# Two cross-attention layers on one core: first-layer probabilities computed a second time with keys on the partitions, in place of transposing them

## The chip, the cores and the metric

The kernel runs on one core of one Trainium2 chip. The metric is the device time in microseconds. The engines are TensorE (PE, its weight loads PEld), VectorE (DVE), ScalarE (ACT), GpSimd (POOL) and SyncE (SP); here SP issues nearly all loads and POOL nearly all stores.

## The reference

Two layers of cross-attention over 8 batches, each with 100 queries of width 640 (20 heads of 32), a context of 722 tokens of width 1024, of which the first 77 are "text" and the other 645 are "ip" tokens. Each layer has two softmaxes per head, one over the 77 text tokens and one over the 645 ip tokens, and adds their results. The first layer, cut to what matters:

```python
text = encoder_hidden_states[:, :TEXT_LEN, :]           # 77 tokens
ip = encoder_hidden_states[:, TEXT_LEN:, :]             # 645 tokens
q = split_heads(hidden_states @ Wq.T)
k, v = split_heads(text @ Wk.T), split_heads(text @ Wv.T)
out_text = merge_heads(softmax(q @ k.T * scale) @ v)
k_ip, v_ip = split_heads(ip @ Wk_ip.T), split_heads(ip @ Wv_ip.T)
out_ip = merge_heads(softmax(q @ k_ip.T * scale) @ v_ip)
out = (out_text + out_ip) @ Wo.T + bo + residual
```

The second layer has the same shape. Its ip scores get an added term from a further text attention, and its ip probabilities are multiplied by a mask per query. All data is float32.

## The kernel before

**Visits.** The attention work is cut into 80 visits (u, c): u from 0 to 15 is a batch in a layer (0 to 7 the first layer, 8 to 15 the second), c from 0 to 4 a chunk of 128 channels, which is four heads. A visit handles 100 queries, four heads, 722 keys.

**What a visit computes.** `scores(u, c, part)` multiplies q and k with the queries on the partitions: part 0 covers keys 0 to 511, part 1 keys 512 to 721 (ip 512 to 644 and the text). Each head lies on 32 partitions of q and k, so four products use four row groups of the array. The results go to two PSUM tiles `sc0` and `sc1` (two heads each, one buffer each), which both parts use in turn. DVE takes the maxima (L1001 of part 0 and 1, L1022 of the text), ACT the exponentials with their sums (L1015), each part under its own maximum. `factors()` (L1037 to L1041) turns the sums and the two maxima into one factor for each query, head and part, and ACT (L1047, `scaled`) and DVE (L1055, L1051, `scaled_rest`) multiply the probabilities p by them. In the following visit, `transposes` (L1096) turns p in six blocks of keys: blocks 0 to 4 of 128 ip keys, block 5 of the last 5 ip keys and the 77 text keys. Each block is four transposes (one per head) and one copy from PSUM to `pt` (L1101 on ACT for blocks 2 and 4, L1103 on DVE for the others). Then `values` (L1119) multiplies `pt` with v, 24 products into one PSUM tile, and DVE copies the result to `hs` (L1123). So a visit holds its own scores and the transposes and values of the visit before.

**Beside it.** Between these pieces PE computes the k and v of the pair of batches that comes next (`psk` L667, `psv` L637), with Strassen-like sums: seven steps a to e in two PSUM buffers, each of them ended by an addition on DVE or a copy on ACT (L202 to L233, the eviction; a step of the first layer's v also evicts a text part, L623 to L627). Some visits also hold pieces of the output product (`pso` L904) and of the next layer's q (`psq` L923).

**Order.** PE, DVE and ACT run in the order in which the program issues their work. The order of a visit is fixed: part 0 of the scores, tasks, transposes 0 and 1, tasks, transposes 2 and 3, part 1, tasks, transposes 4 and 5, tasks, values. `spread` decides how many product tasks fall into each gap: it takes a fixed own time per visit (5.3) and levels the sums. Work on ACT and DVE that follows the scores is put on a list `later` and issued piece by piece, one piece in front of each product task (`emit(1)` in `next_task`), or all of it at fixed places. The queues of SP and POOL are ordered by a scheduler that goes by modelled times. Loads of k (`load_k`, two buffers), v (`load_v`, two buffers) and blocks of the context (`load_x`, three places) are all in SP's queue. The probabilities p have two buffers, `pt` has one.

Of the kernel before, what the change touches and what calls it, by code (L numbers as in the profile page):

```python
# [14 lines left out]
P = 128  # L15
B = 8
# [30 lines left out]
def two_layer_xattn(  # L47
# [35 lines left out]
    k_d = [dram.tile([P, NC_, NI], F32, tag=f"k_{u}", name=f"k_d{u}") for u in range(NU)]  # L83
    v_d = [dram.tile([NB * P, C], F32, tag=f"v_{u}", name=f"v_d{u}") for u in range(NU)]
    g_d = [dram.tile([2, NI, NT], F32, tag=f"g_{g}", name=f"g_d{g}") for g in range(B // 2)]

    ident = const.tile([P, P], F32, tag="ident", name="ident")
    make_identity(nc, ident)
# [876 lines left out]
        nc.sync.dma_start(out[LAST[i] % B], resg[g][:, i])  # L965


    pr, stats, sct = {}, {}, {}

    later = []  # L970

# [8 lines left out]
    def scores(u, c, part):  # L980
        k0, k1 = ((0, KA), (KA, NK))[part]
        if part == 0:
            pr[u, c] = ppool.tile([S, 4, NK], F32, tag="p", name=f"p_{u}_{c}")

            stats[u, c] = stat.tile([S, 14, 4], F32, tag="st", name=f"st_{u}_{c}")
        else:
            free_scores()

        scs = [ps_sc.tile([P, 2, 512], F32, tag=f"sc{h}", name=f"sc_{u}_{c}_{part}_{h}") for h in range(2)]
        for i in range(4):  # L990
            rows = slice(32 * i, 32 * i + 32)
            nc.tensor.matmul(  # L992
                scs[i // 2][:S, i % 2, : k1 - k0], lhsT=qs_[u][rows, c, :], rhs=ks[u, c][rows, k0:k1], start=True, stop=True
            )
        p, st, l = pr[u, c], stats[u, c], u // B
        n = min(k1, NI) - k0
        lo, f, rz, mul = st[:, 6, :], st[:, 7:9, :], st[:, 9:11, :], st[:, 11:13, :]

        def maxima(h):
            if l == 0:  # L1000
                nc.vector.tensor_reduce(  # L1001
                    st[:, part, 2 * h : 2 * h + 2], scs[h][:S, :, :n], AX.X, ALU.max, negate=True
                )
                return
            for i in (2 * h, 2 * h + 1):

                nc.vector.tensor_tensor_reduce(  # L1007
                    out=p[:, i, k0 : k0 + n], in0=scs[h][:S, i % 2, :n], in1=sems[u][:, k0 : k0 + n], scale=-1.0,
                    scalar=3.0e38, op0=ALU.add, op1=ALU.min, accum_out=st[:, part, i : i + 1],
                )  # L1010

        def exponentials(h):
            for i in (2 * h, 2 * h + 1):
                dst = p[:, i, k0 : k0 + n]
                nc.scalar.activation(  # L1015
                    dst, dst if l else scs[h][:S, i % 2, :n], AF.Exp, bias=st[:, part, i : i + 1],
                    scale=-1.0 if l else 1.0, accum_out=st[:, 3 + part, i : i + 1],
                )

        def text_maxima(h):  # L1020
            heads = slice(2 * h, 2 * h + 2)
            nc.vector.tensor_reduce(st[:, 2, heads], scs[h][:S, :, n:KB], AX.X, ALU.max, negate=True)  # L1022
            nc.vector.tensor_tensor(
                p[:, heads, NI:], scs[h][:S, :, n:KB], st[:, 2, heads].unsqueeze(2).to_broadcast([S, 2, NT]), ALU.add
            )

        def differences():

            nc.vector.tensor_tensor(lo, st[:, 0, :], st[:, 1, :], ALU.min)
            nc.vector.tensor_tensor(f, lo.unsqueeze(1).to_broadcast([S, 2, 4]), st[:, 0:2, :], ALU.subtract)  # L1030

        def text_exponentials():
            nc.scalar.activation(f, f, AF.Exp)
            nc.scalar.activation(p[:, :, NI:], p[:, :, NI:], AF.Exp)

        def factors():
            nc.vector.tensor_reduce(st[:, 5, :], p[:, :, NI:], AX.X, ALU.add)  # L1037
            nc.vector.tensor_tensor(st[:, 3:5, :], st[:, 3:5, :], f, ALU.mult)
            nc.vector.tensor_tensor(st[:, 4, :], st[:, 3, :], st[:, 4, :], ALU.add)
            nc.vector.reciprocal(rz, st[:, 4:6, :])  # L1040
            nc.vector.scalar_tensor_tensor(  # L1041
                mul, f, mask_sb[:, l : l + 1], rz[:, 0:1, :].to_broadcast([S, 2, 4]), ALU.mult, ALU.mult
            )

        def scaled(heads):
            for i in heads:
                nc.scalar.activation(p[:, i, :KA], p[:, i, :KA], AF.Copy, scale=mul[:, 0, i : i + 1])  # L1047

        def scaled_rest(text):
            if text:  # L1050
                nc.vector.tensor_tensor(  # L1051
                    p[:, :, NI:], p[:, :, NI:], rz[:, 1, :].unsqueeze(2).to_broadcast([S, 4, NT]), ALU.mult
                )
            else:
                nc.vector.tensor_tensor(  # L1055
                    p[:, :, KA:NI], p[:, :, KA:NI], mul[:, 1, :].unsqueeze(2).to_broadcast([S, 4, NI - KA]),
                    ALU.mult,
                )

        for h in range(2):  # L1060
            maxima(h)
        if part == 0:
            later.append((True, lambda: exponentials(0)))
            later.append((True, lambda: exponentials(1)))
        else:
            for h in range(2):
                text_maxima(h)
            differences()
            later.append((True, lambda: (exponentials(0), exponentials(1), text_exponentials())))
            if (u, c) == ORDER[-1]:  # L1070

                later.append((False, lambda: (
                    factors(), scaled((0, 1)),
                    nc.vector.tensor_tensor(
                        p[:, 2:, :KA], p[:, 2:, :KA], mul[:, 0, 2:].unsqueeze(2).to_broadcast([S, 2, KA]), ALU.mult
                    ),
                    scaled_rest(False), scaled_rest(True),
                )))
                return
            later.append((False, lambda: (factors(), scaled_rest(False))))  # L1080
            later.append((False, lambda: (scaled((0, 1)), scaled_rest(True))))
            later.append((False, lambda: scaled((2, 3))))

    pts = {}

    def transposes(u, c, j, at_end=False):
        if j == 0:
# [17 lines left out]
    def values(u, c):  # L1105
        g, at = group_of[u]
        if g not in hsg:

            hsg[g] = one.tile([P, 2, NC_, S], F32, tag="hs" if g < len(PAIRS) - 1 else "qst", name=f"hs_{g}")
        pt = pts[u, c]  # L1110
        ps = ps_pt.tile([P, 512], F32, tag="pt", name=f"pv_{u}_{c}")
        for j in range(6):
            for i in range(4):
                if j < 5:
                    lhs = vs[u, c][:, j, i * D : (i + 1) * D]
                else:
                    lhs = vts[u][:, (4 * c + i) * D : (4 * c + i + 1) * D]
                rows = P if j < 5 else NTAIL
                nc.tensor.matmul(  # L1119
                    ps[32 * i : 32 * i + 32, :S], lhsT=lhs, rhs=pt[:rows, j, i * S : (i + 1) * S],  # L1120
                    start=(j == 0), stop=(j == 5),
                )
        nc.vector.tensor_copy(hsg[g][:, at, c, :], ps[:, :S])  # L1123


    AHEAD = 1.2
# [63 lines left out]
    def spread(a, b, tasks):  # L1190

        parts = [(max(a, n), min(b, n + 1)) for n in range(math.floor(a), math.ceil(b))]
        own = [(hi - lo) * (5.3 + small_time(math.floor(lo))) for lo, hi in parts]
        total = sum(t for t, _ in tasks)
        level = (total + sum(own)) / (b - a)
        while True:
            room = [max(0.0, level * (hi - lo) - o) for (lo, hi), o in zip(parts, own)]
            if sum(room) <= total * 1.001:
                break
            level *= 0.999  # L1200
        placed, done, i, before = [], 0.0, 0, 0.0
        scale = sum(room) / total
        for t, f in tasks:
            at = done * scale
            while i < len(parts) - 1 and at >= before + room[i]:
                before += room[i]
                i += 1
            lo, hi = parts[i]
            placed.append((t, lo + (hi - lo) * min(1.0, (at - before) / max(room[i], 1e-9)), f))
            done += t  # L1210
        return placed
# [74 lines left out]
    with tc.manual_schedule(engines=PINNED):  # L1286
# [45 lines left out]
        for n, (u, c) in enumerate(ORDER):  # L1332
# [3 lines left out]
            if n == len(ORDER) - 1:  # L1336
                load_v(*last)
                load_v(u, c)
            between(n, 0.0, 0.4, at[0])
            if last:  # L1340
                transposes(*last, 0)
                transposes(*last, 1)
            between(n, 0.4, 0.6, at[1])
            if last:
                transposes(*last, 2)
                transposes(*last, 3)
            scores(u, c, 1)
# [7 lines left out]
            if n + 1 < len(ORDER):  # L1355
                load_k(*ORDER[n + 1])
            if last:
                transposes(*last, 4)
                transposes(*last, 5)
            if few:  # L1360
                between(n, 0.6, 0.8, at[2])
# [58 lines left out]
```

## Time and profile before

| what | value |
|---|---|
| median of 3 runs | 2047.32 us (2045.9 to 2048.35) |
| the profiled execution | 2048.29 us, its span 2046.5 us |
| granted TensorE clock | 0.998 |
| PE, DVE, ACT, POOL busy | 2027.1, 1130.6, 783.0, 274.1 us |
| first-layer visits (0,0) to (7,4) | 405.26 to 1338.82 us of the span |
| PE busy in them | 932.44 of 933.56 us |
| p's transposes (L1096), all visits | 1920, 211.5 us on PE |
| scores (L992), all visits | 1280 instructions, 138.6 us on PE |
| scaling of p on ACT (L1047) | 318 of 713 ns |
| copies to pt: DVE L1103, ACT L1101 | 319 of 568 ns, 161 of 491 ns |

The busy time of a group is the union of its instructions' times; mean ns is that of one instruction. Products that run side by side on several row groups have a mean much longer than their share of the busy time. A float32 product is two instructions in the trace, a transpose is one. "Idle before" is the engine's idle time ahead of a group and what ended it.

### The profile page before, as it was taken

To read this page: it belongs to the slowest core of one execution; us is meant where nothing else is said; L and a number is where in the kernel's file an instruction comes from. 1 tells how busy PE (TensorE), PEld (TensorE's weight loads), DVE (VectorE), ACT (ScalarE), POOL (GpSimd) and SP (SyncE) were. 2 spreads that over 40 slices of the span, in tenths; PEclk is the share of its full clock that TensorE was granted. 3 is DMA by queue.
4 is the path that set the end of the run, shared out by engine and by line. 5 is a ranking of instruction groups with operands and counts; after the bars stand their busy time and mean duration, and the time that the engine had idled before them with its cause. 6 is when DMAs were issued, how large, how long until landed. Compare 5 with 4: busy or idle time off the path is not lost.

```text
span 2046.5 us, 38708 instructions
## 1 busy us (share of the span) xinstructions
PE 2027.1 (99%) x15162; PEld 1573.3 (77%) x15162; DVE 1130.6 (55%) x3047; ACT 783.0 (38%) x2245; POOL 274.1 (13%) x433
## 2 busy tenths in 40 slices
PE   9999999999999999999999999999999999999998
PEld 9676768776876867778678777777777778888877
DVE  2223322246555455554657665656665667778787
ACT  1001000033433343333434344444543545556675
POOL 0001212111111101111111001001011111111110
PEclk9999999999999999999999999999999999999999
DMA  9544323323432533225245353326332535555461
GB/s 343 151 135 147 102 75 93 99 74 90 117 99 74 155 95 110 86 89 166 79 136 162 106 155 113 95 91 180 107 106 89 152 105 152 161 141 139 124 184 52
DMA packets 296484, 252.20 MB, mean 123 GB/s; under 512 B 46638, under 2 KB 265442, under 8 KB 296302
## 3 DMA queue, kind: packets, MB, share of 16 engines
q1 hardware_dynamic: 274254, 181.19, 31.9%
q0 software_dynamic: 21776, 68.44, 9.2%
q8 instruction: 119, 1.95, 0.4%
q14 instruction: 63, 0.52, 0.1%
q10 hardware_dynamic: 272, 0.10, 0.0%
HBM read 180.74 MB, written 68.93 MB: 122 GB/s over the span
## 4 chain that ended last, share of the span: by engine, by line
PE 95%; DVE 4%; ACT 1%; issue 0%; DMA 0%; SPq 0%; DVEq 0%
PE psv_a L637 9%; PE psv_d L637 8%; PE pspt L1096 8%; PE psk_a L667 8%; PE psk_d L667 7%; PE sc L992 6%; PE pv L1119 4%; PE psv_e L637 4%; PE psk_b L667 4%; PE psk_c L667 4%; PE psv_b L637 4%; PE psv_c L637 4%; PE psk_e L667 4%; PE pso L904 3%; PE psq L923 2%; PE psq L305 2%
## 5 line engine op out<-in xcount | busy, mean ns | idle before, releaser
L1015 ACT ACTIVATE p<-sc,st 100x512 f32<-100x512 f32 (+1 forms) x320 | 165.5, 529 | 202.3 <-DVE st L1001 120.5
L1047 ACT ACTIVATE p<-p,st 100x512 f32<-100x512 f32 x318 | 206.7, 713 | 50.9 <-DVE st L1041 50.6
L1096 PEld LDWEIGHTS pspt<-ident,p 100*128 100x128 f32 (+1 forms) x1920 | 189.0, 138 | 43.3 <-issue 5.5
L1103 DVE COPY pt<-pspt 128x400 f32<-128x400 f32 (+1 forms) x319 | 175.3, 568 | 83.8 <-PE pspt L1096 75.3
L1096 PE MATMUL pspt<-ident,p 100*128 100x100 f32 (+1 forms) x1920 | 211.5, 252 | 6.8 <-DVE pt L1103 2.1
L1015 ACT ACTIVATE p<-p,st 100x512 f32<-100x512 f32 (+1 forms) x320 | 176.6, 554 | 78.2 <-DVE st L1007 78.1
L637 PE MATMUL psv_a<-wv,x 128*128 128x397 f32 (+1 forms) x560 | 185.8, 474 | 0.6 <-DVE ko L228 0.3
L1101 ACT COPY pt<-pspt 128x400 f32<-128x400 f32 x161 | 79.1, 491 | 268.4 <-PE pspt L1096 268.0
L637 PE MATMUL psv_d<-wv,s 128*128 128x320 f32 (+1 forms) x560 | 174.5, 454 | 0.0
L691 POOL DMA_DIRECT2D k_d<-ko x140 | 100.0, 718 | 453.5 <-DVE ko L228 399.8
L637 PEld LDWEIGHTS psv_a<-wv,x 128*128 128x128 f32 x560 | 103.2, 190 | 68.5 <-issue 13.3
L1007 DVE CUSTOM_DVE_ANT_0 p<-sc,sem 100x512 f32<-100x512 f32 (+1 forms) x320 | 138.7, 490 | 21.9 <-PE sc L992 21.0
L637 PEld LDWEIGHTS psv_d<-wv,s 128*128 128x128 f32 x560 | 103.8, 190 | 51.8 <-issue 2.5
L1001 DVE TENSOR_REDUCE st<-sc 100x2 f32<-100x1024 f32 (+1 forms) x160 | 125.3, 824 | 28.8 <-PE sc L992 28.7
L992 PE MATMUL sc<-k,q 32*100 32x210 f32 (+1 forms) x1280 | 138.6, 502 | 0.0
L667 PE MATMUL psk_d<-s,wk 128*128 128x256 f32 (+1 forms) x672 | 136.7, 349 | 0.1
L667 PE MATMUL psk_a<-x,wk 128*128 128x256 f32 (+1 forms) x672 | 135.2, 346 | 0.0
L667 PEld LDWEIGHTS psk_d<-s,wk 128*128 128x128 f32 x672 | 108.6, 189 | 20.6 <-issue 6.7
L667 PEld LDWEIGHTS psk_a<-x,wk 128*128 128x128 f32 x672 | 109.6, 189 | 17.6 <-issue 4.5
L652 POOL DMA_DIRECT2D v_d<-vo x70 | 38.8, 554 | 624.6 <-DVE gst L627 318.6
L637 PE MATMUL psv_e<-wvt,x 128*128 128x397 f32 (+1 forms) x280 | 92.9, 474 | 0.0
L1119 PEld LDWEIGHTS pv<-pt,v 128*32 128x32 f32 x3200 | 67.7, 110 | 26.0 <-issue 16.3
(218 smaller groups left out, 3306.0 us busy)
## 6 DMA issues: line engine op xcount, KB each, us to landing
x<-ip_t SPq DMA_DIRECT2D x80, 512.0 KB
k<-k_d SPq DMA_DIRECT2D x80, 322.5 KB
v<-v_d SPq DMA_DIRECT2D x80, 320.0 KB
v_d<-vo POOLq DMA_DIRECT2D x70, 320.0 KB, 2.4
k_d<-ko POOLq DMA_DIRECT2D x112, 128.0 KB, 4.1
o<-wo SPq DMA_DIRECT2D x35, 320.0 KB
x<-ip_t SPq DMA_DIRECT2D x20, 532.0 KB
q<-wq SPq DMA_DIRECT2D x20, 320.0 KB
```

The costliest lines, as they stand in the source:

```text
L637: nc.tensor.matmul(ps[:, :m], lhsT=tokens(k)[:, :P], rhs=w[:, k, :], start=(k == 0 and not go_on), stop=(k == HK - 1), skip_group_check=True,)
L667: nc.tensor.matmul(ps[:, i * m : (i + 1) * m], lhsT=w[:, k, :], rhs=tokens(k), start=(i == 0 and k == 0 and not go_on), stop=(k == HK - 1) ...
L691: nc.gpsimd.dma_start(dst[:, :, r], src)
L992: nc.tensor.matmul(scs[i // 2][:S, i % 2, : k1 - k0], lhsT=qs_[u][rows, c, :], rhs=ks[u, c][rows, k0:k1], start=True, stop=True)
L1001: nc.vector.tensor_reduce(st[:, part, 2 * h : 2 * h + 2], scs[h][:S, :, :n], AX.X, ALU.max, negate=True)
L1007: nc.vector.tensor_tensor_reduce(out=p[:, i, k0 : k0 + n], in0=scs[h][:S, i % 2, :n], in1=sems[u][:, k0 : k0 + n], scale=-1.0, scalar=3.0e ...
L1015: nc.scalar.activation(dst, dst if l else scs[h][:S, i % 2, :n], AF.Exp, bias=st[:, part, i : i + 1], scale=-1.0 if l else 1.0, accum_out= ...
L1047: nc.scalar.activation(p[:, i, :KA], p[:, i, :KA], AF.Copy, scale=mul[:, 0, i : i + 1])
L1096: nc.tensor.transpose(ps[:rows, i * S : (i + 1) * S], pr[u, c][:, i, j * P : j * P + rows], ident[:S, :S])
L1101: nc.scalar.copy(dst, src)
L1103: nc.vector.tensor_copy(dst, src)
L1119: nc.tensor.matmul(ps[32 * i : 32 * i + 32, :S], lhsT=lhs, rhs=pt[:rows, j, i * S : (i + 1) * S], start=(j == 0), stop=(j == 5),)
```

## The change

In the first layer (u below 8), p is no longer scaled and its blocks 0 to 4 are no longer transposed. Instead:

- `finished` runs after part 1: it computes the factors, scales only block 5's part of p (5 ip keys and the text), and stores 8 numbers per query to DRAM: the negated maximum over both parts and the inverse of the sum, each for four heads (`st_d`, alternating between two tensors).
- `load_stats` loads them back in the next visit, from SP's queue: the maxima spread over all 128 partitions, the inverse of each head over that head's 32 partitions. They land in the space of p (which now has 128 partitions) that is free by then.
- `key_scores` computes the scores again in the place of transposes 0 and 1, with keys on the partitions: 5 blocks by 4 heads, k as the weights and q moving. The results lie in the same two PSUM tiles that the two parts of the scores use. For each pair of heads, DVE adds the maxima (128x1000) and ACT takes the exponential, into `pt`.
- `values` sums blocks 0 to 4 and block 5 apart; DVE multiplies the first by the inverse and adds the second.
- `spread` takes 4.6 as the own time of a first-layer visit.

The first scores, their maxima, exponentials and sums stay; so do the transposes of block 5, and the whole second layer.

```diff
+    st_d = [dram.tile([2, 4, S], F32, tag=f"st_{i}", name=f"st_d{i}") for i in range(2)]
...
-            pr[u, c] = ppool.tile([S, 4, NK], F32, tag="p", name=f"p_{u}_{c}")
+            wholes[u, c] = ppool.tile([P, 4, NK], F32, tag="p", name=f"p_{u}_{c}")
+            pr[u, c] = wholes[u, c][:S]
...
+        def finished():
+
+            factors()
+            nc.vector.tensor_tensor(
+                p[:, :, P * NB : NI], p[:, :, P * NB : NI],
+                mul[:, 1, :].unsqueeze(2).to_broadcast([S, 4, NL]), ALU.mult,
+            )
+            scaled_rest(True)
+            nc.sync.dma_start(st_d[(NC_ * u + c) % 2].rearrange("r i q -> q r i"), st[:, 8:10, :])
...
             later.append((True, lambda: (exponentials(0), exponentials(1), text_exponentials())))
+            if l == 0:
+                later.append((False, finished))
+                return
...
+    def load_stats(u, c):
+
+        whole, src = wholes[u, c], st_d[(NC_ * u + c) % 2]
+        nc.sync.dma_start(whole[:, :, :S], src[0].unsqueeze(0).to_broadcast([P, 4, S]))
+        for i in range(4):
+            nc.sync.dma_start(
+                whole[32 * i : 32 * i + 32, :, S : S + S // 4],
+                src[1, i].rearrange("(a q) -> a q", a=4).unsqueeze(0).to_broadcast([32, 4, S // 4]),
+            )
+
+    def key_scores(u, c):
+
+        emit(len(later))
+        pts[u, c] = one.tile([P, 6, 4 * S], F32, tag="pt", name=f"pt_{u}_{c}")
+        scs = [ps_sc.tile([P, 2, 512], F32, tag=f"sc{h}", name=f"sck_{u}_{c}_{h}") for h in range(2)]
+        for j in range(NB):
+            for i in range(4):
+                rows = slice(32 * i, 32 * i + 32)
+                nc.tensor.matmul(
+                    scs[i // 2][:, i % 2, j * S : (j + 1) * S], lhsT=ks[u, c][rows, j * P : (j + 1) * P],
+                    rhs=qs_[u][rows, c, :], start=True, stop=True,
+                )
+
+        def exponentials(h):
+            dst = pts[u, c][:, :NB, 2 * h * S : 2 * (h + 1) * S]
+            nc.vector.tensor_tensor(
+                dst.rearrange("p j (i q) -> p i j q", q=S),
+                scs[h][:, :, : NB * S].rearrange("p i (j q) -> p i j q", q=S),
+                wholes[u, c][:, 2 * h : 2 * h + 2, :S].unsqueeze(2).to_broadcast([P, 2, NB, S]), ALU.add,
+            )
+            nc.scalar.activation(dst, dst, AF.Exp)
+
+        for h in range(2):
+            later.append((True, lambda h=h: exponentials(h)))
...
+                q0 = S if apart and j == 5 else 0
                 nc.tensor.matmul(
-                    ps[32 * i : 32 * i + 32, :S], lhsT=lhs, rhs=pt[:rows, j, i * S : (i + 1) * S],
-                    start=(j == 0), stop=(j == 5),
+                    ps[32 * i : 32 * i + 32, q0 : q0 + S], lhsT=lhs, rhs=pt[:rows, j, i * S : (i + 1) * S],
+                    start=(j == 0 or q0 > 0), stop=(j == 5 or apart and j == 4),
                 )
-        nc.vector.tensor_copy(hsg[g][:, at, c, :], ps[:, :S])
+        hs = hsg[g][:, at, c, :]
+        if apart:
+            nc.vector.tensor_tensor(
+                hs.rearrange("p (a q) -> p a q", a=4), ps[:, :S].rearrange("p (a q) -> p a q", a=4),
+                wholes[u, c][:, :, S : S + S // 4], ALU.mult,
+            )
+            nc.vector.tensor_tensor(hs, hs, ps[:, S : 2 * S], ALU.add)
+        else:
+            nc.vector.tensor_copy(hs, ps[:, :S])
...
-        own = [(hi - lo) * (5.3 + small_time(math.floor(lo))) for lo, hi in parts]
+        own = [(hi - lo) * ((4.6 if lo < NC_ * B else 5.3) + small_time(math.floor(lo))) for lo, hi in parts]
...
+            first = last and last[0] < B
+            if first:
+                load_stats(*last)
             between(n, 0.0, 0.4, at[0])
-            if last:
+            if first:
+                key_scores(*last)
+            elif last:
                 transposes(*last, 0)
                 transposes(*last, 1)
             between(n, 0.4, 0.6, at[1])
-            if last:
+            if last and not first:
                 transposes(*last, 2)
                 transposes(*last, 3)
             scores(u, c, 1)
...
             if last:
-                transposes(*last, 4)
+                if not first:
+                    transposes(*last, 4)
                 transposes(*last, 5)
```

More of the change, by code (lines that the diff above doesn't have):

```diff
@@ L965, in last_out_add @@
         nc.sync.dma_start(out[LAST[i] % B], resg[g][:, i])
-    pr, stats, sct = {}, {}, {}
+    pr, stats, wholes = {}, {}, {}
     later = []
@@ L996, in scores @@
         n = min(k1, NI) - k0
-        lo, f, rz, mul = st[:, 6, :], st[:, 7:9, :], st[:, 9:11, :], st[:, 11:13, :]
+        lo, f, rz, mul = st[:, 8, :], st[:, 6:8, :], st[:, 9:11, :], st[:, 11:13, :]
         def maxima(h):
@@ L1111, in values @@
         ps = ps_pt.tile([P, 512], F32, tag="pt", name=f"pv_{u}_{c}")
+        apart = u < B
         for j in range(6):
```

## The prediction

> **What bounds the kernel now.** I read the page first: busy shares, then the chain that ended last.
>
> ```profile
> span 2046.5 us, 38708 instructions
> ...
> PE 2027.1 (99%) x15162; PEld 1573.3 (77%) x15162; DVE 1130.6 (55%) x3047; ACT 783.0 (38%) x2245; POOL 274.1 (13%) x433
> ...
> PE 95%; DVE 4%; ACT 1%; issue 0%; DMA 0%; SPq 0%; DVEq 0%
> ```
>
> TensorE is busy 99% of the span and 95% of the chain. A share is a mean over stages, so I asked for the busy times of the stretch that the change touches (the 40 first-layer visits, 405.26 to 1338.82 us) and for PE's waits inside it.
>
> ```profile
> core 0: us, PE busy (x) PEld busy (x) DVE busy (x) ACT busy (x) POOL busy (x), PEclk, DMA share, GB/s
> ...
> 405.26:1338.82 933.56, 932.44 (x6746) 708.21 (x6745) 527.86 (x1239) 370.59 (x1087) 126.03 (x202) 1.00 0.38 110
> ```
>
> ```profile
> PE psv_a L637 <- DVE ko L228: 0.3, 1, 0.3
> PE pspt L1096 <- DVE res L909: 0.2, 1, 0.2
> ```
>
> PE idles 1.1 us in 933.6. So only PE time counts here: a microsecond of PE work taken away is a microsecond won, a new PE wait is a microsecond lost, and DVE, ACT and DMA count only through waits that they put on PE. What separates PE from such waits is read in the timeline, here the shortest first-layer visit, (2,3).
>
> ```profile
> 722.12 1.12 PE L992 MATMUL sc<-k,q 32*100 32x512 f32 x8
> ...
> 723.17 2.42 PE L637 MATMUL psv_c<-wvt,x 128*128 128x320 f32 x8
> ...
> 725.43 0.85 PE L1096 MATMUL pspt<-ident,p 100*128 100x100 f32 x8
> ...
> 726.11 2.86 PE L637 MATMUL psv_d<-wv,s 128*128 128x397 f32 x8
> ...
> 727.11 0.21 ACT L1015 ACTIVATION_READ_ACCUMULATOR p<-sc,st 100x1 f32 x1
> ...
> 728.81 0.85 PE L1096 MATMUL pspt<-ident,p 100*128 100x100 f32 x8
> ...
> 729.01 0.49 DVE L222 TENSOR_TENSOR vo<-psv_d,vo 128x320 f32<-128x320 f32 x1 [1.33 <-PE psv_d L637]
> ...
> 729.42 0.23 DVE L625 COPY gst<-psv_d 128x77 f32<-128x77 f32 x1
> ...
> 729.60 0.61 PE L992 MATMUL sc<-k,q 32*100 32x210 f32 x8
> ```
>
> The second part of the scores starts at 729.60 into the same two PSUM tiles whose exponentials ended at 727.3: 2.3 us to spare in the tightest visit. Eight transposes take 0.68 us from start to next start (725.43 to 726.11), 85 ns each.
>
> [...]the 32x100 load of sc takes 160 ns, the 100-column load of psm 168. [...]eight sc products of 502 ns mean come one set in 1.05 us (722.12 to 723.17). [...]DVE's rows stand in program order. [...]
>
> **The change, part by part**, for 40 visits, in the instruction order of the changed program.
>
> *PE, removed.* Blocks 0 to 4, four heads: 20 transposes a visit, 800 x 85 ns = 68 us. Block 5's four stay.
>
> *PE, added.* 20 second scores a visit, 40 instructions (each f32 product is two), weights 32x128, 100 columns moving, four row groups at once: 10 rounds. A round's length isn't shown. Moving 100 columns takes 85 ns (as the transposes)[...]. Nearest row: L956, 128-column weights with 100 moving:
>
> ```profile
> 2016.36 2.40 PE L956 MATMUL pso_last<-hs,wol 128*128 128x100 f32 x20
> 2018.68 1.07 PE L1119 MATMUL pv<-pt,v 128*32 128x100 f32 x40
> ```
>
> 2.32 us for 20, 116 ns. I take 10 x 116 + 0.35 for entering and leaving the tiled group (sc's 210-column set takes 0.54 us for 2 x 175 ns, and its successor's first product 0.1 more) = 1.5 us, 60 us in all. Low end 10 x 85 + 0.3 = 1.15 (46 us); high end 1.75 (70 us), if loads do not overlap. PE work: -8 us (-22 to +2).
>
> *DVE and ACT, off the path as sums.* Per visit DVE loses three copies (L1103, 570 ns) and L1055 (712), gains two additions of 128x1000, one more operation at PV's result (260) and a small scaling. An addition: 421 ns at 256 columns and 491 at 320 (L207, L222) give 1.09 ns a column, so 1.23 us (L1001 reads 1024 in 1.22). Net +0.5 us of a 23 us visit. ACT loses four scalings (714) and two copies (491), gains two exponentials of about 1.1 us: -1.6. Both are idle over 40% of the stretch; cover holds. What matters is where they stand.
>
> *New wait A: the second part of the scores.* Second scores use the two score tiles between the two parts, so part 1 must wait for both additions. They are emitted one per product task: head pair 0's before the first task, pair 1's before the second. **With only one task in between, pair 1's addition stands in DVE's FIFO behind that task's eviction, which waits for the task's end.** PE then waits 0.20 (end to eviction, 728.81 to 729.01) + 0.41 + 0.23 where the text part is evicted too + 1.23 + about 0.1 = 1.9 to 2.2 us. In the changed order this is so in 13 visits: (0,3), (1,2), (1,3), (2,3), (3,3), (4,3), (5,3), (5,4), (6,3), (6,4), (7,1), (7,2), (7,4). 13 x 2.0 = 26 us. About 15 others have two pieces of which the second lasts 1.7 us against the 2.0 needed: 4 us; (7,3), with two block sums of 0.7 us in between, 1.2. Sum 31 us (24 to 38).
>
> *New wait B: the second scores themselves.* They need the tiles when the first part's exponentials are done, and stand where the first transposes stood (which needed only ps_pt). In (2,3), (4,3), (6,3) one task of 2.13 us comes before: PE would be there at 725.4, exponentials end at 727.3, 1.9 us. In (6,4) that task's copy also stands in ACT's queue: 2.8. Sum 8 us (6 to 10). Others have two to four tasks, 4.3 us and more, against 4.2.
>
> *New wait C: the maxima by way of DRAM.* The first addition waits for a store and a load on SP's queue, and all of DVE's queue, the task evictions first, waits behind it. Chain from the end of part 1: factors done after 4.8 us (visit (7,0): 1243.84 to L1041's end 1248.65), two scalings 0.6, the store of 800 four-byte elements, the load. By the page's stores (1.9 to 6.6 us to landing)[...] I estimate 6 (3 to 9) and 3.5 (2.5 to 6): landed after 15 (11 to 20). Wanted: summing PE's own durations from part 1 to the end of the next visit's second scores gives 16 to 23 us in 36 visits, 13.5 to 14.7 in (0,1), (2,4), (4,4), 10.6 plus wait B in (6,4), each with 1.2 us more before PE notices. So 3 us in all; at 20 us most visits lose about 1: 40.
>
> *SP's queue.* Six DMAs a visit, 240. K's load now waits for the second scores (two buffers): issued near the middle of the visit, at least 9 us ahead of its use; in (2,3) before, it was issued at 730.30 and used at 737.05 without a wait. V is read at the end of the next visit. Block loads that end up behind the store have over 20 us (issued 697.00 and 706.29, first read 732.37). I cost these at nothing. What is queued behind the store's wait is then at worst late by the rest of one visit.
>
> *Spacing (4.6 for 5.3).* It moves one task across a border in five of the visits from (8,0) on: nothing.
>
> Sum against the profiled execution's 2048.3 us: -8 + 31 + 8 + 3 = +34, 2082; its time is 1 us above the median of 2047.3, so 2081.
>
> **Rivals.** (1) *PE's saving wins* (faster). The round is 85 ns: 22 us are saved at the second scores. It decides if waits A to C stay below 22 us, for A under about 1 us a single-task visit. For it: the removed work is certain, and four-row tiling does work in sc. Against: A's order in DVE's queue is fixed, and 1.23 us of it is the addition alone. About 2040. (2) *The round trip is late*: first additions wait for DMA in most visits and every eviction with them; at 20 us 2120, at 25 us five more for 40 visits, 2300. For it: 800 four-byte elements, none seen before; against: the slack above. (3) *Waits and savings cancel*: 22 saved, 24 lost: 2049.
>
> **How the numbers follow.** Main case 0.72 (2060 to 2105, likeliest 2081); rival 2 0.16; rival 1 0.08; rival 3 0.04. Range 2057 to 2120: it takes the main case with its bounds and half of rival 2. About 0.2% (4 us) is what a measurement of this kernel can tell from no change; slower 0.88, same 0.04, faster 0.08.
>
> **What would show it.** In the changed profile: second scores of 1.5 us a visit; PE idle in the first layer up from 1 to over 35 us, ended by DVE pt (the additions) ahead of part 1 of the scores in the thirteen visits and by ACT p ahead of the second scores in four; visit (2,3) near 18 us instead of 14.9; hardly any DVE idle ended by a DMA. I am wrong if PE's idle there stays under 20 us, if a round takes 85 ns, or if the additions wait for DMA in most visits.

## The result, and the profile after

The changed kernel takes 2099.12 us (median of 4 runs, 2097.04 to 2107.21) against 2047.17 us for the kernel before (4 runs): a ratio of 1.0261 (95% interval 1.0233 to 1.0289). It is slower, as forecast, and 18 us slower than the 2081 us that the sum gave. The profiled execution took 2097.04 us, its span 2095.3 us, with a granted clock of 0.990 where it was 0.998.

The page of the changed kernel: the span, the engines' busy times, and the chain that ended last by engine.

```profile
span 2095.3 us, 40740 instructions
...
PE 2047.6 (98%) x15962; PEld 1561.0 (75%) x15962; DVE 1147.6 (55%) x3047; ACT 727.9 (35%) x2085; POOL 273.9 (13%) x433
...
PE 90%; DVE 5%; DMA 3%; ACT 1%; issue 1%; DVEq 0%; SPq 0%; ACTq 0%
```

PE's busy time grew by 20.5 us although work was taken from it; DVE and, newly, DMA stand in the chain. The same stretch as before, the 40 first-layer visits, in the windows view of the changed kernel:

```profile
core 0: us, PE busy (x) PEld busy (x) DVE busy (x) ACT busy (x) POOL busy (x), PEclk, DMA share, GB/s
404.83:1389.53 984.70, 956.12 (x7527) 700.69 (x7526) 545.02 (x1238) 314.17 (x927) 126.03 (x202) 0.98 0.52 114
```

The stretch is 51.1 us longer (984.7 for 933.6); all else in the span is 2.3 us shorter. PE is idle for 28.6 us in it instead of 1.1. That is only 27.5 of the 51.1 us. The other 23.7 us are PE busy longer, and the column to look at is PEclk: 0.98 where it was 1.00. PE's waits in the stretch (the waits view: engine, line waited for, total, times, longest):

```profile
PE sc L994 <- DVE pt L1126: 21.3, 23, 1.4
PE sck L1119 <- ACT p L1017: 6.8, 8, 1.2
```

These are the waits A (and C) and B of the prediction, at their places. PE's rows of visit (2,3), from the timeline of the changed kernel (start, length, line, tile, count, and in brackets the idle time before it with its releaser):

```profile
729.76 1.12 PE L994 MATMUL sc<-k,q 32*100 32x512 f32 x8
730.81 2.42 PE L638 MATMUL psv_c<-wvt,x 128*128 128x320 f32 x8
733.83 0.47 PE L1119 MATMUL sck<-q,k 32*128 32x100 f32 x4 [0.59 <-ACT p L1017]
735.16 1.36 PE L1119 MATMUL sck<-q,k 32*128 32x100 f32 x36 [0.87 <-ACT p L1017]
736.45 2.94 PE L638 MATMUL psv_d<-wv,s 128*128 128x397 f32 x8
739.32 0.60 PE L994 MATMUL sc<-k,q 32*100 32x210 f32 x4
741.32 0.60 PE L994 MATMUL sc<-k,q 32*100 32x210 f32 x4 [1.39 <-DVE pt L1126]
741.85 4.63 PE L638 MATMUL psv_e<-wvt,x 128*128 128x397 f32 x8
```

Read the last three lines together. Part 1 of the scores ran in two sets of four products, 0.60 us each, where all eight side by side took 0.61: the split costs 0.6 us that no wait shows. Between the sets PE waits 1.39 us for pair 1's addition. And then the eight products of `psv_e`, of the same form as `psv_d` above (2.94 us), take 4.63 us. Nothing is late in that row. The windows view over those microseconds shows why:

```profile
741.85:742.35 0.50, 0.50 (x3) 0.38 (x2) 0.39 (x2) 0.39 (x1) 0.00 (x0) 0.66 0.06 20
742.35:745.35 3.00, 3.00 (x6) 1.50 (x5) 2.65 (x9) 1.97 (x10) 0.00 (x0) 0.50 0.01 3
745.35:746.35 1.00, 1.00 (x5) 0.50 (x4) 0.00 (x0) 0.00 (x0) 0.00 (x0) 0.96 0.00 0
```

PEclk (third column from the end) is 0.50: the clock was halved for 3.41 us, from 742.01 to 745.43 in the trace's record of the clock. There are 12 such stretches of 3.41 us in the changed kernel's first layer and none in that of the kernel before; each takes 1.7 us, as `psv_e` did here (4.63 us for 2.94), 20.5 us in all. The cost of the split sets is read from the groups of part 1's products, before and after (busy time, mean ns of one):

```profile
L992 PE MATMUL sc<-k,q 32*100 32x210 f32 x640 | 49.2, 377 | 0.0
L994 PE MATMUL sc<-k,q 32*100 32x210 f32 x640 | 60.7, 376 | 21.5 <-DVE pt L1126 21.3
```

That is 11.5 us. The second scores, split in four visits, are busy 55.4 us in this first layer, and 53.7 in the run below where none of them is split (e8): 1.7 us more. So the 51.1 us are: half clock 20.5, idle 27.5, split sets about 13, and PE's own work, about 10 us less (below): together 51.

### The profile page after: what moved, and what is told of

The parts are those of the page before. It is cut to its first block, busy times and chain, and to the rows that moved or that the text cites. A ratio compares the mean times of both kernels' runs of the same rounds, so it can differ in the third digit from the quotient of the medians.

```text
span 2095.3 us, 40740 instructions
## 1 busy us (share of the span) xinstructions
PE 2047.6 (98%) x15962; PEld 1561.0 (75%) x15962; DVE 1147.6 (55%) x3047; ACT 727.9 (35%) x2085; POOL 273.9 (13%) x433
## 4 chain that ended last, share of the span: by engine, by line
PE 90%; DVE 5%; DMA 3%; ACT 1%; issue 1%; DVEq 0%; SPq 0%; ACTq 0%
PE psv_d L638 8%; PE psk_d L668 8%; PE psv_a L638 7%; PE psk_a L668 7%; PE sc L994 6%; PE psv_e L638 4%; PE pspt L1146 4%; PE pv L1172 4%; PE psk_c L668 4%; PE psk_b L668 4%; PE psk_e L668 3%; PE psv_b L638 3%; PE psv_c L638 3%; PE pso L905 3%; PE sck L1119 2%; DMA st_d<-st 2%
## 5 line engine op out<-in xcount | busy, mean ns | idle before, releaser
L638 PE MATMUL psv_d<-wv,s 128*128 128x320 f32 (+1 forms) x560 | 180.0, 465 | 0.0
L994 PE MATMUL sc<-k,q 32*100 32x210 f32 (+1 forms) x1280 | 150.1, 502 | 21.5 <-DVE pt L1126 21.3
L1131 ACT ACTIVATE pt<-pt 128x1000 f32<-128x1000 f32 x80 | 83.0, 1037 | 251.8 <-DVE pt L1126 251.7
L1009 DVE CUSTOM_DVE_ANT_0 p<-sc,sem 100x512 f32<-100x512 f32 (+1 forms) x320 | 138.7, 490 | 21.1 <-PE sc L994 20.1
L668 PE MATMUL psk_d<-s,wk 128*128 128x256 f32 (+1 forms) x672 | 142.5, 360 | 0.0
L1153 DVE COPY pt<-pspt 128x400 f32<-128x400 f32 (+1 forms) x199 | 110.1, 567 | 45.6 <-PE pspt L1146 43.0
L1146 PE MATMUL pspt<-ident,p 100*128 100x100 f32 (+1 forms) x1120 | 127.4, 251 | 7.0 <-DVE pt L1153 2.1
L1146 PEld LDWEIGHTS pspt<-ident,p 100*128 100x128 f32 (+1 forms) x1120 | 109.2, 135 | 30.7 <-issue 4.2
L1126 DVE TENSOR_TENSOR pt<-sck,p 128x1000 f32<-128x1000 f32 x80 | 95.2, 1194 | 64.1 <-DMA p<-st_d 37.3
L1049 ACT ACTIVATE p<-p,st 100x512 f32<-100x512 f32 x158 | 102.8, 713 | 30.1 <-DVE st L1043 29.8
L638 PE MATMUL psv_e<-wvt,x 128*128 128x397 f32 (+1 forms) x280 | 98.3, 495 | 0.0
```

The source lines that it names most:

```text
L638: nc.tensor.matmul(ps[:, :m], lhsT=tokens(k)[:, :P], rhs=w[:, k, :], start=(k == 0 and not go_on), stop=(k == HK - 1), skip_group_check=True,)
L668: nc.tensor.matmul(ps[:, i * m : (i + 1) * m], lhsT=w[:, k, :], rhs=tokens(k), start=(i == 0 and k == 0 and not go_on), stop=(k == HK - 1) ...
L994: nc.tensor.matmul(scs[i // 2][:S, i % 2, : k1 - k0], lhsT=qs_[u][rows, c, :], rhs=ks[u, c][rows, k0:k1], start=True, stop=True)
L1009: nc.vector.tensor_tensor_reduce(out=p[:, i, k0 : k0 + n], in0=scs[h][:S, i % 2, :n], in1=sems[u][:, k0 : k0 + n], scale=-1.0, scalar=3.0e ...
L1126: nc.vector.tensor_tensor(dst.rearrange("p j (i q) -> p i j q", q=S), scs[h][:, :, : NB * S].rearrange("p i (j q) -> p i j q", q=S), whole ...
L1146: nc.tensor.transpose(ps[:rows, i * S : (i + 1) * S], pr[u, c][:, i, j * P : j * P + rows], ident[:S, :S])
```

## The experiments

Three theories. **Order**: the waits stem from where the additions stand (A), where the second scores stand (B), and little from the round trip (C). **Round trip**: the maxima come late from DRAM, for DVE's idle time says so. **Work**: the second scores are dearer than the transposes, for PE's busy time rose. A fourth came from the reading above, **clock**: a wait also costs the half-clock stretch that may follow it. The line for the round trip, from DVE's waits in the changed kernel's first layer:

```profile
DVE pt L1126 <- DMA p<-st_d: 37.3, 12, 6.4
```

### Idle work on TensorE (e3)

`LONE` lists the thirteen single-task visits of the prediction.

```diff
+    def fill(visit, n):
+        ps = ps_pt.tile([P, 512], F32, tag="pt", name=f"fill_{visit[0]}_{visit[1]}_{n}")
+        for _ in range(n):
+            nc.tensor.matmul(ps[:, :S], lhsT=ident, rhs=ident[:, :S], start=True, stop=True)
...
+            if i == 2 and part == 1 and (u, c) in LONE:
+                fill((u, c), 4)
...
+                if (i, j) == (2, 0) and now in ((2, 3), (4, 3), (6, 3), (6, 4)):
+                    fill(now, 2)
```

> Idle work is added to TensorE and nothing is taken away: in the 13 single-task visits four products of the identity with itself (128x128 by 100 columns, some 0.23 us each) between the first and second head pair of part 1 of the scores, and two of them between the head pairs of the second scores in (2,3), (4,3), (6,3), (6,4); nobody reads their result. Clock theory[...]: 9 to 11 of the 12 windows go, the waits stay as long as they are: 2099 - 17 = 2082 (2077 to 2088). Waiting theory (the waits alone are the loss, the half-clock records follow from something else): no gain; 60 products of 0.23 us lie in the waits or add up to 5 us: 2098 to 2105, and the half-clock windows stay.

Measured: 2081.14 us, ratio to before 1.0162 (1.0146 to 1.0177): 18 us faster than the changed kernel, with 60 products more. The same visit in its timeline, and its first layer in the windows view:

```profile
735.26 0.60 PE L1003 MATMUL sc<-k,q 32*100 32x210 f32 x4
735.79 1.14 PE L976 MATMUL fill<-ident 128*128 128x100 f32 x8
737.26 0.60 PE L1003 MATMUL sc<-k,q 32*100 32x210 f32 x4 [0.33 <-DVE pt L1137]
737.79 2.94 PE L638 MATMUL psv_e<-wvt,x 128*128 128x397 f32 x8
```

```profile
405.21:1371.93 966.72, 953.66 (x7646) 702.78 (x7646) 544.86 (x1238) 314.07 (x927) 126.36 (x202) 1.00 0.50 116
```

The second set of scores starts 2.00 us after the first, as in the changed kernel (739.32 to 741.32): the wait is as long as it was, only filled. But `psv_e` is back at 2.94 us, and one half-clock stretch is left of 12. So the clock's share is shown, 18 us of the total, by a run that takes away neither a wait nor any work of the changed kernel.

### Half of that work (e10)

> As the run with idle work on TensorE, with half of it: two products instead of four in the 13 single-task visits, one instead of two in the four visits of the second scores. The gaps ahead of part 1 keep some 0.9 us instead of 0.4. If a window halves the next one's clock only from an idle time of 1.1 us on (none of some 100 windows with 0.2 to 1.1 us of idle did so in the traces so far), this is as fast as the full filler but for late-maxima windows: 2083 (2080 to 2088). If every microsecond of idle counts in proportion, half of the 18 us gained are lost: 2090.

Measured: 2081.31 us, 1.0164 (1.0149 to 1.0180), the same as with the full filler. PE's idle time is more than in that run, as these waits of the half filler's first layer show (8.0 and 2.7 us in those two lines there), and it costs nothing:

```profile
PE sc L1003 <- DVE pt L1137: 13.2, 18, 2.9
PE sck L1130 <- ACT p L1026: 4.0, 8, 0.8
```

This is what the first of the two readings expected (2083), where loss in proportion would have given 2090. So the clock was not lost in proportion to the idle time here; the last section counts how much idle time stood ahead of the half-clock stretches.

### Additions together (e1)

```diff
-        for h in range(2):
-            later.append((True, lambda h=h: exponentials(h)))
+        later.append((True, lambda: (exponentials(0), exponentials(1))))
```

> Both additions of a visit (head pairs 0 and 1) are put into DVE's queue together, before the first product task that follows the second scores; nothing else changes. Order theory (the 13 visits with one task between second scores and part 1 lose because pair 1's addition stands behind that task's eviction): their gaps of 1.3 to 1.4 us and the 0.6 us by which part 1 runs in two sets instead of one go, some 26 us less 3 that belong to late maxima, and with them 8 or 9 of the 12 half-clock windows of 3.41 us, each 1.7 us: 2099 - 38 = 2061 (2052 to 2070), PE gaps in the first layer from 28.6 us to under 14. Round-trip theory (additions wait for the maxima from DRAM): no gain beyond 5 us, 2094 or more. Work theory (second scores are dearer PE work than the transposes, since PE busy rose by 24 us): no gain, 2095 or more.

Measured: 2068.62 us, 1.0105 (1.0088 to 1.0122), 30.5 us faster than the changed kernel. In the profiles the first layer is 31.3 us shorter: half clock 15.4 (9 of the 12 stretches), idle 11.7, split sets the rest. Visits such as (1,2) and (3,3), 3.4 us longer in the changed kernel, are now 0.2 us shorter than before. The gain is within the range expected, but 8 us short of its middle: where the maxima are late, both additions are now late, and (2,4) rose from 23.73 to 24.72 us.

### Two tasks, then three, ahead of the second scores (e5, e9)

Both have the additions together; the diff is the further edit of the run with two tasks. With three, the loop runs on until 6.4 us of product work stand ahead.

```diff
...
+            start = done[0]
             between(n, 0.0, 0.4, at[0])
+            while first and todo[done[0]][1] < n + 1.0 and sum(t > 1.5 for t, _, _ in todo[start : done[0]]) < 2:
+                next_task()
```

> As the run with the additions together; besides, the second scores wait in the program until two product tasks stand before them in the visit, which moves one task ahead of them in (2,3), (4,3), (6,3) and (6,4), and nothing elsewhere. Order theory: wait B (6.2 us of gaps ahead of and inside the second scores there, 1.4 us of split sets, one half-clock window of 1.7 us) goes: 2068.6 - 9 = 2060 (2056 to 2063). Rival: the moved task was the cover of part 1's own exponentials, and the next visit's scores or PV wait instead: 2066 or more.

> As the run with the additions together, but the second scores wait in the program until product work of at least 6.4 us by the plan's own durations (three tasks) stands before them in the visit. Nothing is left out and the one store stays where the changed kernel has it. If wait C is the rest of the loss (2058.9 us with two tasks against 2045.4 without the round trip), a third task gives the maxima 2 us more in the tight visits, and most of the 13.5 us go: 2048 (2044 to 2053), half-clock windows in the first layer none or one. If the third task only moves the wait (part 1's exponentials, which then lack their cover before the next visit's scores), 2056 or more.

Two tasks: 2058.91 us, 1.0054 (1.0041 to 1.0067). Wait B is down to 0.3 us, as expected. Its four runs also show the clock at work within one kernel: 2053.46 us at a granted clock of 1.000, 2058.01 and 2059.81 at 0.997, 2062.53 at 0.995. Three tasks: 2056.97 us, 1.0050 (1.0038 to 1.0063), no measurable step further: the expected 2048 failed, and its rival, that the wait only moves, fits. DVE's idle time for the maxima fell from 27.6 to 15.0 us, but PE's wait for the additions hardly (8.4 to 7.1 us): it went from (2,4), (4,4) and most of (6,4), and new ones stand in (3,0), (5,0) and (7,1).

### The round trip taken out (e2, e8)

```diff
...
-        whole, src = wholes[u, c], st_d[(NC_ * u + c) % 2]
+        n = NC_ * u + c
+        whole, src = wholes[u, c], st_d[(n - 2 if n > 1 else n) % 4]
```

> The loads take the maxima and inverse sums that the visit two before had stored, through four DRAM tiles instead of two; the first two visits take their own. The exponents and factors of the first layer are therefore those of another visit. Everything else, stores and loads and additions, is as in the changed kernel, but no addition can wait for the round trip. Round-trip theory: the 37.3 us of DVE idle ended by this load all reach PE: 2062 or below. Order theory: only (0,1), (2,4), (4,4), (6,4), (7,1), (7,2) gain, gaps of 0.5 to 1.3 us each, 5 to 6 us, 2 us of split sets, and two or three half-clock windows of 1.7 us: 2099 - 11 = 2088 (2083 to 2094); the 1.3 us gaps ahead of part 1 in the other single-task visits stay.

> Additions together, two tasks ahead of the second scores, and the loads take the maxima and inverse sums of the visit two before (the first layer's exponents and factors are those of another visit). No wait of the three kinds is left by construction, so that the difference to the kernel before is the PE work term alone: 2047.5 - 8 = 2040 (2026 to 2050 by the prediction's bounds). Work theory (second scores dearer): 2055 or more.

From the changed kernel alone (e2): 2083.65 us, 1.0176 (1.0161 to 1.0191). The round-trip theory wanted 2062; the order theory's 2083 to 2094 just holds it. DVE's idle time for the load fell from 37.3 to 2.3 us, and of these 35 us the first layer gave back 17.9: half clock 12.0, idle 4.2, split sets 1.7.

With the additions together and two tasks besides (e8), 1.0 us is left of the waits A to C: 2045.37 us, 0.9990 (0.9982 to 0.9998), within the 2026 to 2050 expected. That refutes the work theory, which wanted 2055 or more. Its first layer, in the windows view and in PE's waits there:

```profile
406.11:1336.44 930.33, 927.21 (x7526) 683.39 (x7525) 543.94 (x1238) 315.63 (x927) 126.02 (x202) 1.00 0.54 121
```

```profile
PE psk_a L668 <- ACT ko L203: 1.6, 2, 0.9
PE sc L994 <- DVE pt L1127: 1.0, 3, 0.5
```

It is 930.3 us, 3.2 shorter than before. PE's instructions are as many as in the changed kernel's (7526 for 7527), and they fit into 927.2 us where they took 956.1. A visit whose tasks are unchanged is 0.25 us shorter than before (17 of the 40 by 0.22 to 0.25), 10 us if all 40 saved as much. The account of the whole first layer comes near: 3.2 us shorter, with 2.0 us more of PE's idle time, and 4.0 us more in the first scores, whose sets are not all side by side even here (`sc` busy 73.3 us for 69.3). The work itself is then 9 us less.

### The maxima stored earlier (e4, e6, e7)

```diff
...
+        def put(k):
+            nc.sync.dma_start(
+                (st_d, rz_d)[k][(NC_ * u + c) % 2][0:1].rearrange("r i q -> q r i"), st[:, 8 + k : 9 + k, :]
+            )
...
             differences()
+            if l == 0:
+                put(0)
...
-            nc.sync.dma_start(st_d[(NC_ * u + c) % 2].rearrange("r i q -> q r i"), st[:, 8:10, :])
+            put(1)
```

> The maxima are stored as soon as the differences are done, some 2 to 3 us earlier than now, with a DMA of their own of 400 elements; the inverse sums follow where the one store is now, to another DRAM tile, and the four loads of them stay. One DMA more a visit. If the six or so late additions cost what the order theory gives them, most of the 11 us of the run with old maxima are won: 2090 (2085 to 2096), and DVE's idle ended by this load falls from 37 to under 15 us. If the store's length or SP's queue and not its start decides (the first load waits behind something else on SP), no gain: 2097 or more.

Measured: 2108.32 us, 1.0297 (1.0282 to 1.0313), 9 us slower than the changed kernel: the expectation failed. The maxima were stored 2.0 us after part 1's end instead of 4.8 (medians), and most visits had them earlier. But SP's queue now stood still more often: in the first layer it waited 125 times for values to store or for a store's landing, 587 us, for 78 times and 560 us in the changed kernel. SP's waits between 1196 and 1222 us of this run, and PE's in its first layer:

```profile
SPq L1114 <- DMA rz_d<-st: 7.0, 1, 7.0
SPq L1112 <- DMA st_d<-st: 4.2, 1, 4.2
SPq L1064 <- DVE st L1033: 4.0, 1, 4.0
```

```profile
PE psq L925 <- DMA q<-wq: 10.3, 4, 4.6
```

For 15 of 26 us SP waits for one of the two stores or for the values to store. The weights of `psq` were queued behind, and PE waited 10.3 us for them, a wait that the changed kernel doesn't have. Its wait for the additions grew too, from 21.3 to 26.2 us.

So the stores went to ScalarE's queue, with the additions together (e6), and with two tasks as well (e7):

```diff
...
-            nc.sync.dma_start(
+            nc.scalar.dma_start(
...
+            scores(u, c, 1)
+            if first:
+                load_inverse(*last)
```

> As the run with the additions together; besides, the maxima have a store of their own, issued from ScalarE's queue ahead of part 1's exponentials, the inverse sums another, later, from ScalarE's queue too, and the four loads of the inverse sums stand behind part 1 of the next visit's scores on SP, so that SP waits for one landing a visit and not for two. Queue theory (the early store lost because SP then stood waiting twice a visit, with weights behind it): the late additions go now, 7.1 us of gaps, about 3 us of split sets, two half-clock windows of 1.7 us: 2068.6 - 12 = 2057 (2052 to 2061), no waits of PE for weights. Rival (the round trip is as long whatever starts it, or ScalarE's exponentials get late behind the store): 2066 or more.

> Additions together, two tasks ahead of the second scores, and the maxima stored early from ScalarE's queue: waits A, B and C all gone, half-clock windows of the first layer gone. If the work term of the prediction is right (-8 us, from -22 to +2), this comes to 2041 and a rest of late maxima to 2044 (2038 to 2052), level with the kernel before or up to 0.4% faster. If the second scores are dearer than the transposes that they replace: 2055 or more.

Measured: 2088.09 us, 1.0201 (1.0186 to 1.0215), and 2088.02 us, 1.0192 (1.0168 to 1.0217), 20 and 29 us slower than the same kernels with the one later store on SP. Both expectations failed. SP still waits for two landings in most visits, as its waits in e7's first layer show (the waits of PE there below them):

```profile
SPq L1111 <- DMA st_d<-st: 395.1, 39, 35.5
SPq L1117 <- DMA rz_d<-st: 153.1, 37, 11.2
```

```profile
PE sc L995 <- DVE pt L1137: 15.4, 11, 3.8
PE sc L995 <- DMA k<-k_d: 3.9, 1, 3.9
PE psq L925 <- DMA q<-wq: 3.1, 2, 2.7
```

In e5 the additions cost PE 8.4 us and loads nothing. Evictions cost it 1.0 us there and 6.6 here. In the profiles e7's first layer is 37.5 us longer than e5's: 21.7 of idle and 15.8 of PE busy longer, mostly at half clock. So the loss is not that of a single wait, and what each part of this edit adds to it stays open. In e7 the typical chain from part 1's end to the landed maxima is shorter (median 14.4 us for 16.2 in e5, by the trace's packets), its longest is longer (22.9 for 20.1). Visit (2,3) is one of the long ones. SP's loads there, and the DMA engines' share and rate (last two columns of the windows view):

```profile
741.32 0.43 SPq L897 DMA_DIRECT2D o<-wo  x1
741.85 0.47 SPq L515 DMA_DIRECT2D v<-v_d  x1
742.42 0.47 SPq L509 DMA_DIRECT2D k<-k_d  x1
742.94 0.63 SPq L510 DMA_DIRECT2D k<-kt_d  x1
756.33 0.37 SPq L1111 DMA_DIRECT2D p<-st_d  x1
```

```profile
744.00:748.00 4.00, 4.00 (x17) 2.27 (x15) 2.67 (x11) 1.97 (x10) 0.74 (x2) 1.00 1.03 329
748.00:752.00 4.00, 4.00 (x63) 2.58 (x63) 2.90 (x7) 0.75 (x2) 0.00 (x0) 1.00 0.83 131
```

The early store is issued at 744.69, 2.3 to 3.4 us after three loads of some 320 KB each, and the load that waits for it is let go only at 756.33, 11.6 us later. In e5 the store of this visit came later against the loads (share of the DMA engines 0.30 in its 4 us) and the same step took 6.5 us. That the bulk loads hold the store up is my reading of these two; no run took the loads away to show it.

## Why the prediction was right, and where it was not

**Side and range** held: slower, 2099 within 2057 to 2120. The side came from the waits that were foreseen. That 2099 also lies in the main case's 2060 to 2105 is in part luck: those bounds were drawn for the waits, and the sum was 18 us short for want of a term for the clock.

**PE's work** (-8, from -22 to +2): measured -9 to -10, by the two accounts of e8. Ten rounds follow each other by 112 ns where 116 was taken, and the second scores take 1.30 us from their start to the next product's, for 1.5. A round's four loads take 187 ns each, so they overlap. The 175 ns that the prediction takes for 210 columns were an estimate; eight 397-column products of `psv_d` take 2.70 us from start to next start (726.11 to 728.81 in the kernel before), 0.85 ns a column, which makes 178.

**Wait A** (+31): the thirteen visits were the right ones, and 2.0 us a visit was right. With the clock kept by the filler, (1,3) and (3,3) are 1.67 us longer than before, (1,2) and (5,3) 1.73 and 1.74; with the 0.25 us of work saved that is 1.9 to 2.0. The further 5 us for visits with two pieces between were too much: of them only (7,3) shows a loss, 0.7 us.

**Wait B** (+8): right. (2,3) and (4,3) with the filler are 18.50 us; their 14.93 before, less 0.25, plus 2.0 for A leaves 1.8 for B, for 1.9 predicted. "Near 18 us" holds with the clock kept; in the changed kernel it was 20.3.

**Wait C** (+3, 0 to 40): about twice as large, 6 us without the clock's part (idle 4.2 and split sets 1.7 in e2). The 3 us were more than the prediction's own figures give for the four visits at a landing of 15 us, which is about 1 us. The trip was under-sized: from store to the load's issue 7.9 us in the median (6.0 to 12.6), 6 predicted; from there to the last packet 4.4 (3.6 to 9.2), 3.5 predicted, by estimate, with no such load in the trace before; landed 17.4 us after part 1's end (14.7 to 22.3), 15 predicted. In the four visits named the first addition starts latest, 2.4 to 4.5 us after the second scores' end; in six others, named nowhere, it is held up to 1.2 to 2.1 us after it. "Hardly any DVE idle ended by a DMA" was wrong: 37.3 us. It was far from all PE's: e2 got back 6 us of PE time for 35 us of DVE idle, before the clock.

**SP's queue at nothing** held for the change as it is: PE waits for no load in its first layer. For a second store it does not hold, as e4 shows.

**The waits together**: predicted 42 us, measured 27.5 idle and about 13 in split sets, 40.5. "PE idle up from 1 to over 35 us" was missed only because a third of that loss isn't recorded as idle: four products alone take as long as eight (0.60 us and 0.61).

**The step that failed**: "a new PE wait is a microsecond lost". It is more than that. In the changed kernel's first layer the trace's record of the clock has 12 stretches of half clock, all of 3.41 us, whose starts lie whole multiples of 3.41 us apart (8, 47, 83 and 122 of them from the first to the next four). PE was idle for 1.17 to 1.81 us in the 3.41 us ahead of each, and the stretch at 608.89 us follows a single gap of 1.33 us. The prediction has no term for the clock. Two fifths of the loss (20.5 of 51.1 us) were the clock, and the filler's run, which has the waits and keeps the clock, stands at 2081.1 us, where the sum without the clock stood. That it stands there so exactly is luck: 5 us too many in wait A, 3 too few in wait C and one or two of work saved cancel in part, and one half-clock stretch is left in that run.

**Loose readings.** The 502 ns of a product of sc are the mean of both its forms; those of the set at 722.12 take 628, so the overlap is larger than was said. Five us more for 40 visits at a trip of 25 us make 2320, not 2300. Neither bears on the sum.

**The rivals.** "PE's saving wins" is what e8 approaches, at -2.3 us, not -7: even with nearly no waits the change gains next to nothing here. "The round trip is late" is a part, not the cause. "Waits and savings cancel" is not met: the waits alone are over four times the work saved. No version run that waits for its own maxima beats the kernel before; the best, with three tasks, is 0.50% slower.

## What to carry to other kernels

Price a wait on TensorE twice: its own length, with the loss of side-by-side running where it splits a set (0.6 us here), and the half-clock stretch that may follow it (1.7 us); then look at PEclk over a few microseconds, not over the stage. Where a wait of a microsecond or two can't be removed, useless work inside it may keep the clock: it won 18 of 51 us here, with the waits as long as before. And before adding an operation behind others in an engine's queue, count what stands between it and its reader in every iteration, not in the mean one: 13 visits of 40 carried wait A.

## What the runs showed of the hardware that was not expected

Half-clock stretches followed idle times well under their own length of 3.41 us: 1.17 to 1.81 us in the changed kernel. I laid the 3.41 us grid, as each trace's half-clock records fix it, over the first layers of the changed kernel and the ten experiments, and summed PE's idle time in each window of the grid that itself had the full clock. In the changed kernel 18 windows have 1.16 to 1.81 us of idle, and 12 of them were followed by half clock; the others all have under 1.1 us, and none was. In all eleven traces, of 144 windows with 0.2 to 1.1 us none was followed by half clock; of 64 with 1.1 to 1.6 us, 20; of 13 with 1.6 to 2.0 us, 7; of 10 with more, all. (Windows already at half clock are left out: six of them, with under 1.1 us of idle, were followed by another.)

Idle time alone does not decide in between. Of the 64 windows, 20 also hold both split sets of part 1 almost whole (over 1.15 of their 1.20 us), four products side by side on two of the four row groups; 16 of these were followed by half clock, and 4 of the other 44. Why is not shown: this is a count made afterwards, and no run changed the sets alone.

The same visit can lie differently on the grid. Visit (1,2) has the same wait of 1.39 us in the changed kernel and in e2, whole inside one window both times. In the changed kernel the two split sets lie in that window too (1.20 us); in e2 its edge cuts them to 0.82 us, and the visit takes 24.79 us for 26.49, without a half-clock stretch.
